# A decoder kernel on one core: other opening order, ternary weights by comparisons, and one projection piece in two parts

## The chip, the cores and the metric

The kernel runs on 1 core of one Trainium2 chip. The metric is the device time of one execution in microseconds. A profiled execution also gives a span, from the first to the last instruction that the profiler shows.

## What is computed

Sixteen sequences of 256 tokens with 512 features pass one decoder layer of three parts, each followed by adding the input and normalising (mean 0, variance 1 over the features).

```python
x = _layernorm(x + _L0_attn_ref(x, w_q, w_k, w_v, w_o), axis=-1)
x = _layernorm(x + _L0_xattn_ref(ctx, ctx, x, ssm_kernel, D, 8), axis=-1)
x = _layernorm(x + _L0_ffn_ref(x, gamma, W), axis=-1)
```

The first part is causal attention with 16 heads of 32, whose four projections are of the "bit" kind:

```python
sw = 1.0 / jnp.clip(jnp.mean(jnp.abs(w)), 1e-05, None)
wq = jnp.clip(jnp.round(w * sw), -1.0, 1.0) / sw
sx = 127.0 / jnp.clip(jnp.max(jnp.abs(x), axis=-1, keepdims=True), 1e-05, None)
xq = jnp.clip(jnp.round(x * sx), -128.0, 127.0) / sx
y = xq @ wq.T
```

So each weight matrix (512 x 512) becomes -1, 0 or 1 times its mean size, which is known only when the whole matrix has been read, and each token becomes integers times its own scale. The second part is a causal convolution of products of the context with a kernel, multiplied with the layer's input; the third is one more such projection with weights W. Both are left alone by the change, except that W's rounding lies in the first part's steps.

## The kernel before, in words

**Attention** works on one sequence (a "batch" b, 256 tokens, two tiles of 128) per step, 16 steps, in a pipeline over batches. Everything is ordered by hand: inside `manual_schedule` each of the five instruction streams (PE, ACT, DVE, POOL, SP) runs in the order in which the source issues it.

In step b the four head groups g are gone through as four rounds. A round is `scan(b+1, g)`, which computes the scores of the next batch to get the row maxima (`nmax`, L311 on DVE), some other PE work, `weigh(b, g)`, which computes the scores transposed with the maxima added (L339, L346), takes the exponential on ACT (L351), masks it on POOL (L355) and adds two parts on POOL (`both`, L361), and more PE work. `scan` and `weigh` use one and the same PSUM tile `s` (4 of 8 banks, one buffer), so a scan waits for the exponentials of the weighing before it, and a weighing for the maxima of the scan before it. `values(b, g)` multiplies probabilities with V (L374) and sums them (L381). All other PSUM tiles ("misc": `total`, `row`, `acc`, `acc_v`, `pv`, `tps`, `ops`, `acc_o`, `tpn`) share three banks in turn.

The PE work between the rounds is the projection of batch b+2: four pieces `project_qk(b+2, i)`, i = 0 and 2 for Q, 1 and 3 for K, each two blocks of 128 features (eight matmuls, L260) that DVE scales out of PSUM with one operation on 512 elements (L264), and two pieces `project_v` (L272, scaled out by ACT, L276). Piece 0 comes after scan 0, pieces 1 and 2 after the weighings 0 and 1, piece 3 after scan 3, the V pieces after scan 2 and weighing 2. Further: `spread` (the token scales as a row, L236, copied by ACT, L238), `lay` (the maxima split in three bf16 terms on DVE, L320 to L323) and `lay_turned` (their transposition on PE, L329, copied by ACT to `low`, L331; `spread` and `weigh` need `low`), `divide`, `out_scales`, `close` (the output projection, L442 to L446), `keep`. Tokens of batch b+3 are loaded, scaled on POOL (L157), rounded on ACT (L163) and transposed by a DMA (L251).

**The opening** is `begin` (L556) and `first_step` (L586), before step 0. The loads are issued first: x[0], w_k, x[1], w_o and w_f on the SP queue, w_q, w_v and two small ones on the ACT queue (L57 to L69). The constants are made on POOL where the source stands (L71 to L104); the scheduler was free to mix them there, since that part is outside `manual_schedule`. A weight matrix i lies as 128 x 2048 f32 in a buffer lent from the later `x1t` tile. It is made ternary in these steps:

1. `weight_size` (L114): the sum of the absolute values per partition, on DVE for w_q (L116) and on ACT for the others (L118).
2. `weight_scale` (L120): a matmul with ones adds over partitions (L123), DVE makes the multiplier (L124, L125), `weight_inverse` its inverse (L127).
3. `weight_round` (L132): multiply and add a magic number (L135), which rounds, then clip (L136): for w_q and w_k in halves on DVE, for the others whole on POOL.
4. `weight_store` (L145): ACT subtracts the magic number and writes bf16 (L147).

The tokens of batches 0 and 1 are turned on PE (`transposed`, L166 to L171) and their scales spread by a matmul with `diag` (L225, L234). Then `first_step` runs the four scans of batch 0, projects batch 1 and V of both, and makes w_v, w_o and a part of w_f ternary. The rest of w_o and w_f follows in step 0 (L512 to L514, L525).

**The second layer** (from L644) goes over 32 heads; nothing in it is changed.

Of the kernel before, what the change touches and what calls it, by code (L numbers as in the profile page):

```python
# [32 lines left out]
def decoder_kernel(ctx: ExitStack, tc: tile.TileContext, x, ctx_t, w_q, w_k, w_v, w_o, ker, d_skip, gamma, w_f, out):  # L33
# [25 lines left out]
    for i, w in enumerate((w_q, w_k, w_v, w_o, w_f)):  # L59
        (nc.scalar, nc.sync, nc.scalar, nc.sync, nc.sync)[i].dma_start(  # L60
            raw[i].rearrange("p (c o) -> p c o", o=E), w.rearrange("(c p) o -> p c o", p=P)
        )
        if i == 1:
            second = xp.tile([P, S // P, E], F32, name="xt")
            nc.sync.dma_start(second, x[1].rearrange("(t p) e -> p t e", p=P))
    rows = lent(6, E + P, XH)
    nc.scalar.dma_start(rows, ker)
    dsk = lent(7, 1, XH)
    nc.scalar.dma_start(dsk, d_skip.rearrange("(h o) -> h o", o=1))  # L69

    ones = const.tile([P, P], F32, name="ones")  # L71
    nc.gpsimd.memset(ones, 1.0)
    ident = const.tile([P, P], F32, name="ident")
    make_identity(nc, ident)
    ident_h = const.tile([P, P], BF16, name="ident_h")
    nc.vector.tensor_copy(ident_h, ident)
    half = const.tile([P, 2], F32, name="half")
    nc.gpsimd.memset(half, -0.5)


    mask_f = lent(7, 3 * P)[:, P : 3 * P].rearrange("p (j k) -> p j k", j=2)
    nc.gpsimd.memset(mask_f, 0.0)
    for j in range(2):
        nc.gpsimd.affine_select(
            out=mask_f[:, j, :], in_=mask_f[:, j, :], compare_op=ALU.is_ge, fill=NEG_INF,
            base=0, pattern=[[-1, P]], channel_multiplier=1,
        )
    mask = const.tile([P, 2, P], BF16, name="mask")


    pick_f = const.tile([P, NB + 1], F32, name="pick_f")
    nc.gpsimd.memset(pick_f, 0.0)
    for base in range(0, P, 8):
        if base % DH != 24:
            nc.gpsimd.affine_select(
                out=pick_f, in_=pick_f, compare_op=ALU.not_equal, fill=1.0,
                base=-base, pattern=[[-1, NB + 1]], channel_multiplier=1,
            )
# [3 lines left out]
    nc.gpsimd.memset(col, 0.0)  # L102
    for g in range(NB):
        nc.gpsimd.memset(col[:, g, g : g + 1], 1.0)  # L104
# [6 lines left out]
    parts = const.tile([P, 5], F32, name="parts")  # L111
    w_mul = const.tile([P, 5], F32, name="w_mul")

    def weight_size(i, engine):  # L114
        if engine is nc.vector:
            nc.vector.tensor_reduce(parts[:, i : i + 1], raw[i], AX.X, ALU.add, apply_absolute_value=True)  # L116
        else:
            nc.scalar.activation(lent(5, W), raw[i], AF.Abs, accum_out=parts[:, i : i + 1])  # L118

    def weight_scale(ps, i):  # L120
        total = ps.tile([P, 1], F32, name="total", tag="misc")
        c = slice(i, i + 1)
        nc.tensor.matmul(total, ones, parts[:, c], start=True, stop=True)  # L123
        nc.vector.tensor_scalar(w_mul[:, c], total, 1.0 / (E * E), 1e-5, ALU.mult, ALU.max if i < 4 else ALU.add)  # L124
        nc.vector.reciprocal(w_mul[:, c], w_mul[:, c])  # L125

    def weight_inverse(i):  # L127
        nc.vector.reciprocal(w_inv[:, i : i + 1], w_mul[:, i : i + 1])
        if i == 0:
            nc.vector.tensor_scalar(q_scale, w_inv[:, 0:1], 1.0 / math.sqrt(DH), None, ALU.mult)  # L130

    def weight_round(i, engine, part, n=2):  # L132

        both = (
            lambda t: engine.tensor_scalar(t, t, w_mul[:, i : i + 1], MAGIC, ALU.mult, ALU.add),  # L135
            lambda t: engine.tensor_scalar(t, t, MAGIC + 1.0, MAGIC - 1.0, ALU.min, ALU.max),  # L136
        )
        if n == 1:
            t = raw[i][:, part * W // 2 : (part + 1) * W // 2]
            both[0](t)  # L140
            both[1](t)
        else:
            both[part](raw[i])

    def weight_store(i, half=None):  # L145
        c = slice(0, W) if half is None else slice(half * W // 2, (half + 1) * W // 2)
# [841 lines left out]
```

## Time and profile before

| | us |
|---|---|
| median of 3 runs | 903.2 (902.22 to 903.83) |
| the profiled execution | 903.6 |
| its span | 901.3 |
| PE busy | 807.7 (90%) |
| DVE busy | 683.3 (76%) |
| POOL busy | 594.2 (66%) |
| ACT busy | 421.4 (47%) |

The profile is of one execution. Its page gives the busy time of each engine, the span in 40 slices of 22.5 us, the DMA queues, the chain of waits that ended last, and the costliest groups of instructions by source line. Apart from the page the trace answers questions: a timeline of single instructions (start, duration, engine, line, output <- input, and in brackets the idle time before it and what ended it), and windows (for each engine the busy time and, in brackets, the number of instructions, in the order PE, PEld, DVE, ACT, POOL, then the granted PE clock, the share of the DMA engines and GB/s). PEld is PE's loading of weights. An engine that is idle costs nothing where another one sets the pace.

### The profile page before, as it was taken

The page shows a single profiled execution, that of the slowest core. Times are in us where ns is not written, and L with a number is a line of the kernel's source. Part 1 is how long each engine was busy: PE and PEld are TensorE (multiplying, and loading weights), DVE is VectorE, ACT ScalarE, POOL GpSimd, SP SyncE. Part 2 cuts the span into 40 slices and gives each one's busy share as a digit, 9 for nine tenths or more (in the row PEclk, how much of TensorE's full clock was granted, in tenths as well). Part 3 has the DMA queues.
Part 4 walks back from the last instruction along what each step waited for, and adds up shares of the span by engine and source line. Part 5 has one row for each costly group of instructions (what it writes and reads, how often), then busy time and mean ns, then how long its engine had stood idle before and what let it go on. Part 6 is the DMA issues. An engine that isn't in the chain of part 4 may idle for free. (4 is left out here: it accounts for less than half of the span.)

```text
span 901.3 us, 20309 instructions
## 1 busy us (share of the span) xinstructions
PE 807.7 (90%) x7784; PEld 577.1 (64%) x7860; DVE 683.3 (76%) x1748; ACT 421.4 (47%) x696; POOL 594.2 (66%) x689
## 2 busy tenths in 40 slices
PE   3788999999999999997668999999999999999991
PEld 2456666666666666665336777777777776767770
DVE  5747777787888777876355788888888887888883
ACT  5463555556555556554442344333444334424432
POOL 3554545454544455443456999999899998998970
PEclk9999999999999999999988999999999999999995
DMA  8012223332222222111140323333223333233201
GB/s 306 1 40 67 65 72 72 71 73 45 47 66 66 67 71 72 49 36 36 38 116 12 82 75 81 86 89 94 83 75 89 84 93 77 76 83 93 65 31 34
DMA packets 103695, 64.91 MB, mean 72 GB/s; under 512 B 68080, under 2 KB 84464, under 8 KB 103600
## 3 DMA queue, kind: packets, MB, share of 16 engines
q1 hardware_dynamic: 102448, 61.45, 25.7%
q10 hardware_dynamic: 1152, 2.18, 0.7%
q8 instruction: 62, 1.02, 0.5%
q14 instruction: 33, 0.27, 0.1%
HBM read 43.34 MB, written 8.47 MB: 57 GB/s over the span
## 5 line engine op out<-in xcount | busy, mean ns | idle before, releaser
L706 PE MATMUL y<-kv,w 128*128 128x288 f32 x1280 | 336.6, 411 | 4.3 <-DVE turn L730 4.0
L706 PEld LDWEIGHTS y<-kv,w 128*128 128x128 f32 x1280 | 234.9, 191 | 65.1 <-issue 8.7
L864 POOL TENSOR_TENSOR own<-own,turn 128x512 f32<-128x512 f32 x128 | 162.9, 1272 | 35.5 <-DVE turn L730 20.2
L355 POOL TENSOR_SCALAR_AFFINE_SELECT p<-p 128x512 f32<-128x512 f32 x128 | 80.9, 656 | 139.2 <-ACT p L351 135.4
L311 DVE TENSOR_REDUCE nmax<-s 128x4 f32<-128x512 f32 (+1 forms) x128 | 116.6, 953 | 63.9 <-PE s L306 62.7
L675 POOL TENSOR_TENSOR kv<-c 128x512 f32<-128x512 f32 (+1 forms) x160 | 148.7, 947 | 2.6 <-DMA c<-in_ctx_t 2.6
L351 ACT ACTIVATE p<-s 128x1536 f32<-128x1536 f32 x64 | 92.9, 1451 | 84.4 <-PE s L346 84.4
L764 ACT ACTIVATE root<-quarter 128x3 f32<-128x3 f32 (+2 forms) x33 | 6.7, 204 | 226.1 <-DVE quarter L759 226.1
L361 POOL TENSOR_TENSOR both<-p 128x512 f32<-128x512 f32 x64 | 81.9, 1280 | 5.3
L717 DVE SCALAR_TENSOR_TENSOR own<-y,q 128x128 f32<-128x128 f32 x128 | 36.0, 281 | 61.4 <-PE y L706 53.9
L866 POOL TENSOR_TENSOR own<-own 128x256 f32<-128x256 f32 x96 | 69.8, 727 | 7.5
L739 PE MATMUL tok<-ident,own 128*128 128x128 f32 x448 | 71.4, 276 | 0.7 <-POOL own L866 0.6
L739 PEld LDWEIGHTS tok<-ident,own 128*128 128x128 f32 x448 | 55.8, 141 | 24.7 <-POOL own L866 6.2
L260 PE MATMUL acc<-xit,w 128*128 128x256 bf16 x512 | 68.4, 279 | 2.4 <-DVE x1t L135 1.3
L720 DVE TENSOR_TENSOR own<-y,q 128x384 f32<-128x384 f32 x128 | 70.0, 547 | 0.2
L730 DVE TENSOR_TENSOR turn<-y,q 128x384 f32<-128x384 f32 x128 | 69.9, 546 | 0.0
L339 PE MATMUL s<-qt,kt 32*128 32x256 f32 (+1 forms) x1024 | 60.6, 350 | 4.9 <-DVE nmax L311 4.8
L306 PE MATMUL s<-kt,qt 32*128 32x128 f32 (+1 forms) x1024 | 60.9, 352 | 0.0
L260 PEld LDWEIGHTS <-w 128*128 128x128 bf16 x512 | 46.0, 100 | 22.8 <-issue 15.4
L339 PEld LDWEIGHTS s<-qt,kt 32*128 32x128 f32 x1024 | 47.7, 186 | 19.7 <-issue 9.1
L374 PE MATMUL pv<-p,va 128*32 128x256 f32 (+1 forms) x1024 | 55.7, 332 | 5.2 <-POOL p L355 5.1
L386 ACT COPY ot<-pv 128x256 f32<-128x256 f32 x64 | 23.8, 372 | 71.9 <-PE pv L374 70.9
(136 smaller groups left out, 1320.4 us busy)
## 6 DMA issues: line engine op xcount, KB each, us to landing
xt<-in_x SPq DMA_DIRECT2D x16, 512.0 KB, 4.6
xr<-in_x SPq DMA_DIRECT2D x16, 512.0 KB, 4.9
c<-in_ctx_t SPq DMA_DIRECT2D x32, 256.0 KB, 3.3
w<-taps SPq DMA_DIRECT2D x32, 256.0 KB, 4.4
out_y<-res SPq DMA_DIRECT2D x32, 256.0 KB, 2.0
c<-in_ctx_t SPq DMA_DIRECT2D x32, 128.0 KB, 3.2
x1t<-in_w_q ACTq DMA_DIRECT2D x1, 1024.0 KB, 9.0
x1t<-in_w_v ACTq DMA_DIRECT2D x1, 1024.0 KB, 14.3
```

The costliest lines, as they stand in the source:

```text
L260: nc.tensor.matmul(acc[:, j, :], w[:, c, o * P : (o + 1) * P], m.xit[:, c].rearrange("p t k -> p (t k)"), start=(c == 0), stop=(c == NB - 1),)
L311: nc.vector.tensor_reduce(m.nmax[:, t, :, g], s[:, :, cols], AX.X, ALU.max, negate=True)
L339: nc.tensor.matmul(s[:, r, lo:hi], m.kt[rows, g, k0 : k0 + P], m.qt[rows, g, q0:S], start=(lo == 0), stop=False, skip_group_check=True,)
L351: nc.scalar.activation(p, s[:, :, 0 : 3 * P], AF.Exp)
L355: nc.gpsimd.affine_select(out=own, in_=own, compare_op=ALU.is_ge, fill=0.0, base=0, pattern=[[0, 4], [1, P]], channel_multiplier=-1,)
L361: nc.gpsimd.tensor_tensor(both, p[:, :, P : 2 * P], p[:, :, 2 * P : 3 * P], ALU.add)
L675: nc.gpsimd.tensor_tensor(kv[:, :, at : at + n * B].rearrange("p c (i b) -> p c i b", b=B), c[:, :, i : i + n, :], c[:, :, i + d : i + d + ...
L706: nc.tensor.matmul(y[:, Y0 + k * HALF : Y0 + (k + 1) * HALF], lhs, kv[:, mb, k * HALF : (k + 1) * HALF], start=(mb == 0), stop=(mb == lb),)
L720: nc.vector.tensor_tensor(own[:, 1:4, :], view(y, Y0 + AT + P, [[P, 3], [1, P]]), view(q, base + B, [[B, 3], [1, P]]), ALU.mult)
L730: nc.vector.tensor_tensor(view(t, B, [[P + B, 3], [1, P]]), view(y, Y0 + AT + P, [[P, 3], [1, P]]), view(q, base, [[0, 3], [1, P]]), ALU.mult,
L739: nc.tensor.matmul(tok[:, lb, :], lhsT=own[:, d, :], rhs=ident, is_transpose=True, start=(d == 4), stop=(d == 0))
L864: nc.gpsimd.tensor_tensor(own[:, 0:4, :], own[:, 0:4, :], turns[lb], ALU.add)
```

## The change

It has five pieces.

- **Loads.** All go on the SP queue, in the order x[0], w_q, w_k, x[1], w_v, w_o, w_f, the convolution kernel, d_skip.
- **Constants.** They are made inside `manual_schedule` in source order: `constants` first in `begin`, `zeros` (zeros of `nmax`, `terms`, `col`) after the scaling of batch 1.
- **Ternary w_q and w_k by two comparisons.** Instead of multiplying, rounding, clipping and storing, `weight_below` marks w < -size/2 (f32, on POOL; for one half of w_q on DVE) and `weight_ternary` computes (w > size/2) - mark on DVE straight into bf16. The size of w_q is taken half on DVE and half on ACT. w_v, w_o and w_f are still rounded, now in halves on POOL.
- **The order of the opening.** The size of w_o moves to the end of `first_step`, that of w_f into step 0; w_o is rounded and stored in step 0, w_f in step 1. The scales and maxima of batch 1 are taken before w_k's ternaries; Q is scaled out of PSUM later.
- **The step.** `project_qk(b+2, 0)` is done in two parts: its first block where it was, its second after the second V piece. `lay_turned(b)` stands after scan 0 of step b instead of at the end of step b-1, and `values(b-1, 3)` ahead of `spread` and the projection.

```diff
-        (nc.scalar, nc.sync, nc.scalar, nc.sync, nc.sync)[i].dma_start(
+        nc.sync.dma_start(raw[i].rearrange("p (c o) -> p c o", o=E), w.rearrange("(c p) o -> p c o", p=P))
...
+    def weight_limit(i, total, above):
+        sign = 1.0 if above else -1.0
+        nc.vector.tensor_scalar(
+            limits[:, i, above : above + 1], total, sign * 0.5 / (E * E), sign * 0.5e-5,
+            ALU.mult, ALU.max if above else ALU.min,
+        )
+    def weight_below(i, half, engine):
+        c = part_of(half)
+        engine.tensor_scalar(below[:, c], raw[i][:, c], limits[:, i, 0:1], None, ALU.is_lt)
+    def weight_ternary(i, half):
+        c = part_of(half)
+        nc.vector.scalar_tensor_tensor(
+            weights[i].rearrange("p c o -> p (c o)")[:, c], raw[i][:, c], limits[:, i, 1:2], below[:, c],
+            ALU.is_gt, ALU.subtract,
+        )
...
+    def project_qk(m, i, blocks=(0, 1), wait=False):
...
         on(scan, b + 1, 0)
-        if b == 0:
-            lay_turned(batches[0], 0)
+        on(lay_turned, b, b)
         on(fetch_x, b + 3, b + 3)
         on(fetch_again, b - 1, b - 1)
+        on(values, b - 1, NB - 1)
         on(spread, b + 2, b + 2)
-        on(project_qk, b + 2, 0)
-        on(values, b - 1, NB - 1)
+        on(project_qk, b + 2, 0, (0,))
...
         on(weigh, b, 0)
+        if b < 2:
+            weight_round(3 + b, 0)
         if b == 0:
-            weight_store(3)
-            weight_round(4, nc.gpsimd, 1)
+            weight_size(4, nc.scalar)
...
         if b == 0:
-            weight_store(4)
+            weight_scale(4, weight_total(ps, 4))
+        if b < 2:
+            weight_round(3 + b, 1)
+            weight_store(3 + b, 0)
...
         on(project_v, b + 2, 1)
+        on(project_qk, b + 2, 0, (1,))
+        if b < 2:
+            weight_store(3 + b, 1)
...
         on(close, b - 1)
-        on(lay_turned, b + 1, b + 1)
...
     def begin():
         m, n = batches[0:2]
+        constants()
         fetch_x(m, 0)
         fetch_x(n, 1)
         fetch_scales(m, 0)
         fetch_scaled(m, 0)
-        nc.vector.tensor_copy(mask, mask_f)
-        weight_size(0, nc.vector)
+        nc.vector.tensor_copy(pick, view(pick_f, 0, [[1, NB + 1], [0, P]]))
+        weight_size(0, nc.vector, 0)
+        weight_size(0, nc.scalar, 1)
+        total = weight_total(ps, 0)
+        weight_limit(0, total, 0)
+        weight_below(0, 1, nc.gpsimd)
+        weight_below(0, 0, nc.vector)
+        weight_limit(0, total, 1)
+        weight_ternary(0, 0)
+        weight_ternary(0, 1)
+        weight_scale(0, total)
         fetch_rounded(m)
         weight_size(1, nc.scalar)
-        weight_scale(ps, 0)
-        spread(m, 0)
         turn_in(m, 0)
-        for half in range(2):
-            weight_round(0, nc.vector, half, 1)
-            weight_store(0, half)
-        weight_scale(ps, 1)
...
+        spread(m, 0)
+        total = weight_total(ps, 1)
+        weight_limit(1, total, 0)
+        weight_below(1, 0, nc.gpsimd)
+        weight_below(1, 1, nc.gpsimd)
+        weight_limit(1, total, 1)
+        weight_scale(1, total)
         fetch_scales(n, 1)
         fetch_scaled(n, 1)
+        weight_ternary(1, 0)
+        weight_ternary(1, 1)
+        zeros()
+        weight_size(2, nc.scalar)
         fetch_rounded(n)
+        q0 = project_qk(m, 0, wait=True)
+        q1 = project_qk(m, 2, wait=True)
+        k0 = project_qk(m, 1, wait=True)
+        q0()
+        k1 = project_qk(m, 3, wait=True)
+        k0()
+        return q1, k1
```

The first step after it, as it stands after the change:

```python
def first_step(q1, k1):
    m, n, o = batches[0:3]
    fetch_x(o, 2)
    q1()
    k1()
    scan(m, 0)
    weight_scale(2, weight_total(ps, 2))
    turn_in(n, 1)
    spread(n, 1)
    for part in range(2):
        weight_round(2, part)
        weight_store(2, part)
    scan(m, 1)
    project_qk(n, 0)
    values_scale(m)
    values_scale(n)
    fetch_scales(o, 2)
    values_scale(o)
    fetch_scaled(o, 2)
    scan(m, 2)
    project_qk(n, 1)
    project_v(m, 0)
    project_v(m, 1)
    fetch_rounded(o)
    turn_in(o, 2)
    weight_size(3, nc.scalar)
    scan(m, 3)
    project_qk(n, 2)
    lay(m, 0)
    project_v(n, 0)
    total = weight_total(ps, 3)
    project_qk(n, 3)
    weight_scale(3, total)
    project_v(n, 1)
    write_taps()
```

## The prediction

> **What bounds the kernel now.** I read the 40 slices first: PE is at 9 tenths in nearly all of them, except the first three (0 to 68 us), the seam between attention and the second layer (425 to 475 us) and the end. The chain of waits that ends last lies in the second layer, which the change does not touch. So two places matter: the opening, and the attention steps as far as PE waits in them.
>
> The timeline of PE gives the steps by their first scan (L299).
>
> ```profile
> 23.09 0.60 PE L299 MATMUL s<-mask,ident_h 128*128 128x256 bf16 x4
> 46.74 1.06 PE L299 MATMUL s<-mask,ident_h 128*128 128x256 bf16 x4
> 51.19 0.94 PE L339 MATMUL s<-qt,kt 32*128 32x256 f32 x16
> 72.51 0.60 PE L299 MATMUL s<-mask,ident_h 128*128 128x256 bf16 x4 [1.16 <-ACT p L351]
> 225.23 0.60 PE L299 MATMUL s<-mask,ident_h 128*128 128x256 bf16 x4
> 250.69 0.60 PE L299 MATMUL s<-mask,ident_h 128*128 128x256 bf16 x4
> ```
>
> The opening takes 46.74 us; step 0 starts there. A later step takes 250.69 - 225.23 = 25.46 us. In it PE waits twice for more than a moment:
>
> ```profile
> 209.67 0.94 PE L339 MATMUL s<-qt,kt 32*128 32x256 f32 x16 [0.23 <-DVE nmax L311]
> 218.76 0.60 PE L299 MATMUL s<-mask,ident_h 128*128 128x256 bf16 x4 [0.64 <-ACT p L351]
> ```
>
> The fourth scan of a step waits 0.64 us for the exponentials, while before the first weighing PE is full (it starts at 228.92 with no wait). In the opening the windows of 2 us show PE nearly idle at 42 to 46 us, and the clock granted afterwards at 0.50; the timeline shows a 0.19 us cast that took 1.90 while POOL ran a rounding of 1.89 us.
>
> ```profile
> 42.00:44.00 2.00, 0.28 (x2) 0.01 (x1) 1.93 (x3) 0.00 (x0) 1.92 (x2) 1.00 0.00 0
> 44.00:46.00 2.00, 0.80 (x3) 0.36 (x3) 1.61 (x7) 0.89 (x2) 1.91 (x4) 0.84 0.00 0
> 46.00:48.00 2.00, 2.00 (x11) 0.90 (x13) 0.00 (x0) 1.64 (x3) 1.66 (x1) 0.50 0.32 66
> 42.34 1.90 DVE L322 CAST terms<-rest 128x40 bf16<-128x40 f32 x1
> ```
>
> **Part 1, the loads.** Before, x[0] (0.52 MB) shares the DMA engines with w_q on the other queue and lands at 6.97; w_q lands at 9.80, w_k at 13.03. Adding the MB moved in the windows of 1 us gives 0.39 by 4 us, 0.65 by 5, 1.45 by 7, 1.86 by 8, 2.59 by 10, 2.99 by 11. On one queue, served in order, x[0] is through at 4.5, x[0] and w_q (1.57) at 7.3, with w_k (2.62) at 10.1. The old landings lie about 1.0 to 1.3 behind such sums (x[0] and an equal part of w_q, 1.05 MB, are through at 6.0; landed 6.97). So I take x[0] at 5.5, w_q at 8.4, w_k at 11.4, x[1] at 13 and w_v at 15.4 (15.6 before). That one queue can carry it is seen at 18 to 19 us, when the other queue has landed its last byte (16.7): 389 GB/s. SP's load of x[2] comes behind the one of d_skip, which waits for x[0] (5.5), and waits itself for POOL's last read of x[0] (8.6); the weights queued ahead take longer.
>
> ```profile
> 18.00:19.00 1.00, 0.74 (x4) 0.56 (x5) 0.97 (x2) 1.00 (x2) 0.00 (x0) 1.00 1.05 389
> ```
>
> **Part 2, up to the first scan.** DVE: amax 1.22 and two of 0.2 from 5.5 give x_m at 7.1 (8.6 before). POOL's constants, in source order, end near 5.4 (12 selections of 0.25 from 2.3), so they delay nothing. POOL then scales x (2 x 0.7) and makes diag (2 x 0.6), to 9.8. The size of w_q: each half takes 2.29/2 on DVE and 1.91/2 + 0.19 on ACT, to 9.7. Two sums on PE (0.74 from DVE's end to the next use, and 0.28 for the second matmul): 10.7.
>
> The two comparisons have no row. `below` is a one-operand DVE operation on 1024 elements (L136: 0.69) or half of POOL's 1.97. Both start at 10.8, one on each engine; after the blocked cast above I let one wait for the other, to 12.5. The ternary combination (L154, two SBUF operands, 1024 elements) lies between 0.69 (L136, one operand) and 1.90 (the cast behind POOL); from 512 elements (L264, 0.75) and 1.1 ns for each more (L720 to L409) I take 1.25. Two of them from 12.5, then two scales: 15.4. Meanwhile ACT sizes w_k from 11.4 (1.91 + 0.19), and only then copies xit (2 x 0.55), at 14.6; the row matmul waits for the first copy (1.0) and w_k's sum follows, so the limits of w_k come at 15.8. POOL's two `below` end at 17.9, DVE meanwhile makes amax of x[1] and x_m; its two tiny ones wait out POOL, 18.4. Two ternaries: 20.9. POOL scales x[1], makes its diag (2.6) and only then the zeros (1.2): 22.3, needed by nmax at 24.2. The rest of K's projection, 0.8, and the second block, 1.05: first scan at 22.7, against 23.0. So up to here the new weights buy almost nothing: four operations of 1.25, three of 1.0 on POOL and one of 0.7 replace eight of 0.7 and four stores on ACT.
>
> The Trainium skill, "SBUF — State Buffer", section "Who interferes with whom", speaks against this: it says that a DVE instruction with two SBUF inputs is locked out while GpSimd reads SBUF, and that the first to issue holds the pair for its whole length. The blocked cast agrees for a one-operand operation; no row here shows two SBUF operands beside POOL. By that rule w_k's ternaries would alternate with POOL's two scalings of x[1] (0.7 each) and the first scan would come at an estimated 23.4 instead of 22.7.
>
> **Part 3, from the first scan to step 0.** Here DVE and ACT gain, since the size of w_o and w_f is no longer taken before w_v is stored (2 x 2.1 on ACT), and w_v is rounded and stored in halves. Before, nmax runs at 25.49, 29.33, 34.42 and 38.65. After: the scales of q1 and k1 first (to 23.9), nmax of scan 0 at 24.2 to 26.0 (amax of x[1] is already done), scan 1 at 26.4 behind turns and row, nmax 27.9 to 29.7, scan 2 at 29.9. DVE then scales q (0.75) and takes amax of x[2] (1.21 + 0.4), so nmax 2 runs 32.1 to 33.9; scan 3 at 34.1, nmax 3 to 37.5. POOL rounds w_v from 26.4 in four pieces to 30.3, ACT stores the last half by 31.4, in time for the V projection at 32.2. ACT: V evictions to 34.9, x[2] rounded to 36.2, size of w_o to 38.3. PE waits for that: sum 38.3, V eviction 39.0, last K projection to 40.1, last V to 41.1. **Step 0 starts at 41.1, 5.6 earlier.** Its first weighing starts 4.45 after its scan before, 3.69 in a later step; the 0.50 clock and the turn, copy and row one after the other made the difference. With the values laid between I take 3.4: 44.5 against 51.19, **6.7 earlier**.
>
> Steps 0 and 1 then carry w_o and w_f: 2.1 for size and 2 x 1.06 of stores on ACT in step 0 (3.8 in two stores before), 2 x 2 of rounding on POOL in each. What hides them: ACT is busy 13.9 of 26 us there (50 to 76), POOL 13.4. Behind ACT's size stand one copy of 0.37 and the next exponential, which needs a weighing that ends 3 us later. POOL's rounding (2.0) ends 0.6 or more before the next selection. If that cover were gone, each piece could cost up to its own 2 us.
>
> **Part 4, the step order, 13 times (steps 1 to 13 project).** Half a projection (0.5 on PE) leaves the stretch between scan 0 and the first weighing and lands behind the second V projection, where PE waits 0.64: all of it fits. The turn (0.11) moves behind scan 0. The first weighing was set by PE, 3.69 after its scan: 3.69 - 0.5 + 0.11 = 3.3. Next is DVE: nmax of scan 0 runs 226.77 to 228.59, right behind the moments of `close` (end 226.67), and a weighing starts about 0.15 after nmax (209.52, 209.67): 3.51, or 3.40 if the earlier scan lets nmax start 0.1 sooner. The values stand directly behind scan 0 now and need POOL's sum `both`, which ends 2.41 after the scan; PE gets there at 2.3, so it waits about 0.15 and that is still inside. The gain is 3.69 less 3.40 to 3.51, 0.2 to 0.3; afterwards all waits shift alike. DVE gains one instruction (0.45 + 0.45 for 0.75), in a stretch where it idles 2.94. Bounds: 0.1 and 0.45. 13 x 0.25 = **3.3**.
>
> **Sum.** The profiled execution took 903.6 (span 901.3), 0.4 above the median of the three runs, 903.2. 6.7 + 3.3 = 10.0; 903.6 - 10.0 = 893.6 for such an execution, **893.2** for the median. Bounds: each of the four ternaries in line by -0.55 or +0.65 (-2.2, +2.6), landings of w_q and w_k by 1 us either way, PE at 0.5 clock in the gap at 18 to 21 us (up to 0.8), steps 1.3 to 5.9: 888.5 to 899.0.
>
> **Rivals.** (a) The comparisons and POOL block each other more, or part 3 hangs longer on ACT (w_o's size before the last projections): the opening gains only 2.7; 903.2 - 2.7 - 3.3 = 897.2. For it: the blocked cast, the long queue on ACT. Against: DVE idles 2.0 to 3.5 us at a time there. (b) The ternaries run in 0.7 and loads come early: 9.5 and 13 x 0.3; 889.8. (c) The step edit does nothing, since DVE's nmax sets the first weighing anyway: 896.5. Against it: the 228.59 above. (d) **Slower**: one queue carries only what is seen at the start (170 GB/s in the window of 3 to 4 us). The 6.9 MB up to x[2] then take 40.6 us and land at 43.6; DVE, in order, holds nmax 2 behind amax of x[2], wanted at 30.5, so all after it comes 13.1 later: 906.3. It decides against the change below some 176 GB/s; 389 at 18 to 19 us speaks against it.
>
> **How the numbers follow.** Forecast 0.58, (a) 0.17, (b) 0.12, (c) 0.08, (d) 0.05. 888.5 to 899.0 takes in all but (d) and tails. About 0.2% (1.8 us) is what a measurement of this kernel can tell from no change. Slower by more: most of (d), 0.04; within: 0.03, the rest of (d) and the tail of (a); faster: 0.93.
>
> **What would show it.** x[0] landing near 5.5 and w_k near 11.4; the first scan near 22.7; step 0 near 41 with the clock at 1.00; steps of 25.1 to 25.3 with no wait above 0.2 at the fourth scan and a wait for nmax before the first weighing; L154 near 1.25. Wrong would be: PE waits for `both` over 0.3 in each step, steps 0 and 1 longer than 25.8, or x[2] landing after 30 us.

## The result, and the profile after

| | before | after |
|---|---|---|
| median of six runs each, us | 903.1 (901.5 to 903.8) | 895.8 (894.4 to 898.8) |
| the profiled execution, us | 903.6 | 897.0 |
| its span, us | 901.3 | 895.3 |
| first scan / step 0 / its first weighing | 23.09 / 46.74 / 51.19 | 26.02 / 43.12 / 46.62 |
| a later step, us | 25.46 | 25.355 |
| start of step 14 | 403.45 | 397.53 |

After takes 0.992 of the time before (95% interval 0.990 to 0.994): 7.3 us faster by the medians, where 9.9 were forecast (893.2). The time lies inside the range, 2.6 above the forecast.

The timeline of PE of the changed kernel, the lines that answer to those of before (L331 is the scan, L371 the weighing):

```profile
26.02 0.60 PE L331 MATMUL s<-mask,ident_h 128*128 128x256 bf16 x4
43.12 0.60 PE L331 MATMUL s<-mask,ident_h 128*128 128x256 bf16 x4
46.62 0.94 PE L371 MATMUL s<-qt,kt 32*128 32x256 f32 x16 [0.55 <-DVE nmax L343]
67.94 0.60 PE L331 MATMUL s<-mask,ident_h 128*128 128x256 bf16 x4 [1.60 <-ACT p L383]
213.69 0.60 PE L331 MATMUL s<-mask,ident_h 128*128 128x256 bf16 x4 [0.20 <-ACT p L383]
220.06 0.60 PE L331 MATMUL s<-mask,ident_h 128*128 128x256 bf16 x4
223.76 0.94 PE L371 MATMUL s<-qt,kt 32*128 32x256 f32 x16
245.41 0.60 PE L331 MATMUL s<-mask,ident_h 128*128 128x256 bf16 x4
```

The first scan comes 2.9 us later than before, not 0.3 earlier; step 0 still comes 3.6 earlier, because all that lies between is shorter. The wait of 0.64 at the fourth scan is down to 0.20, as forecast, and yet a step is only 0.1 shorter: the first weighing comes 3.70 after its scan, as before (3.69).

The start of step 14 is the mark by which I compare profiles: what lies behind it is the second layer, touched by no kernel here, and the last two steps, in which only the two moves apply (the last output projection ends 63.8 us behind the mark, before and after). All this took 493.1 to 497.9 us from one profile to the next, so a single span says little below 5 us. Up to it the changed kernel gains 403.45 - 397.53 = 5.9: 3.6 up to step 0, 0.95 in step 0 (25.77 to 24.82, with the clock at 1.00 where it was 0.50 to 0.84; from its scan to its turn 1.40 us instead of 2.34), and 13 x 0.105 = 1.4 in the steps. The other 1.4 us by which the medians differ is within the scatter and is put down to nothing here.

Where the opening lost time is seen in the timelines of POOL, DVE and PE from 10 to 24 us:

```profile
10.51 3.40 POOL L150 TENSOR_SCALAR x1t<-x1t,limits 128x1024 f32<-128x1024 f32 x1 [1.31 <-DVE limits L143]
15.65 5.66 POOL L150 TENSOR_SCALAR x1t<-x1t,limits 128x1024 f32<-128x1024 f32 x2 [1.74 <-DVE limits L143]
10.46 0.75 DVE L150 TENSOR_SCALAR x1t<-x1t,limits 128x1024 f32<-128x1024 f32 x1
11.31 1.95 DVE L154 SCALAR_TENSOR_TENSOR w<-x1t,limits 128x1024 bf16<-128x1024 f32 x1
13.95 1.28 DVE L154 SCALAR_TENSOR_TENSOR w<-x1t,limits 128x1024 bf16<-128x1024 f32 x1 [0.69 <-POOL x1t L150]
18.53 2.13 DVE L154 SCALAR_TENSOR_TENSOR w<-x1t,limits 128x1024 bf16<-128x1024 f32 x1 [1.31 <-POOL x1t L150]
21.35 1.70 DVE L154 SCALAR_TENSOR_TENSOR w<-x1t,limits 128x1024 bf16<-128x1024 f32 x1 [0.69 <-POOL x1t L150]
20.72 0.39 PE L290 MATMUL acc<-xit,w 128*128 128x256 bf16 x2 [1.79 <-DVE w L154]
23.11 3.08 PE L290 MATMUL acc<-xit,w 128*128 128x256 bf16 x14 [2.00 <-DVE w L154]
```

A comparison (`below`, L150) takes 0.75 on DVE and 2.83 on POOL (3.40 beside DVE's), where I had put 1.0. DVE waits for POOL ahead of three of the four ternary operations, and PE waits for DVE ahead of K's projection. Then the projection itself is slow: 14 matmuls in 3.08 us, 0.22 each, with the granted clock down to 0.51. The windows of 2 us, the PE clock in the third column from the end:

```profile
22.00:24.00 2.00, 0.89 (x5) 0.65 (x6) 1.71 (x2) 0.99 (x2) 2.00 (x2) 0.64 0.00 1
24.00:26.00 2.00, 2.00 (x11) 1.45 (x10) 1.39 (x2) 0.27 (x1) 1.83 (x13) 0.51 0.00 0
```

### The profile page after: what moved, and what is told of

Read it like the earlier page. It is cut to its first block, busy times and chain, and to the rows that moved or that the text cites. A ratio compares the mean times of both kernels' runs of the same rounds, so it can differ in the third digit from the quotient of the medians.

```text
span 895.3 us, 20336 instructions
## 1 busy us (share of the span) xinstructions
PE 811.7 (91%) x7785; PEld 576.3 (64%) x7862; DVE 687.4 (77%) x1756; ACT 419.0 (47%) x697; POOL 605.5 (68%) x698
## 5 line engine op out<-in xcount | busy, mean ns | idle before, releaser
L290 PE MATMUL acc<-xit,w 128*128 128x256 bf16 x512 | 72.1, 282 | 4.3 <-DVE w L154 3.8
L371 PE MATMUL s<-qt,kt 32*128 32x256 f32 (+1 forms) x1024 | 60.6, 350 | 5.2 <-DVE nmax L343 5.2
L371 PEld LDWEIGHTS s<-qt,kt 32*128 32x128 f32 x1024 | 47.7, 186 | 20.1 <-issue 9.3
```

Source lines behind the costliest of these rows:

```text
L290: nc.tensor.matmul(acc[:, j, :], w[:, c, o * P : (o + 1) * P], m.xit[:, c].rearrange("p t k -> p (t k)"), start=(c == 0), stop=(c == NB - 1),)
L371: nc.tensor.matmul(s[:, r, lo:hi], m.kt[rows, g, k0 : k0 + P], m.qt[rows, g, q0:S], start=(lo == 0), stop=False, skip_group_check=True,)
```

## The experiments

The theory after the result: POOL's comparisons, 1.8 us each dearer than I took them, make the opening late; in the step the turn (`lay_turned`), put ahead of the first weighing, takes back most of what the split gives: by its own 0.22 us and by starting 1.40 us after the scan, where the row started 1.29 after it (the 0.11 that the expectations call the change of rows). Rivals: the ternary operations, or what the new order and the loads do otherwise, make the opening late; in the step, the split itself gives little. Medians are of 4 to 12 runs, ratios to runs of the kernel before on the same chip; the marks from "first scan" on are from one profile of each.

| run | what differs from after | median, us | ratio to before (95%) | first scan | step 0 | per step | step 14 |
|---|---|---|---|---|---|---|---|
| after | | 895.84 | 0.992 (0.990 to 0.994) | 26.02 | 43.12 | 25.355 | 397.53 |
| e1_below_dve | comparisons on DVE | 893.20 | 0.989 (0.986 to 0.992) | 22.34 | 39.43 | 25.355 | 394.01 |
| e2_round_dve | old rounding of w_q, w_k | 890.45 | 0.986 (0.983 to 0.989) | 21.23 | 38.33 | 25.355 | 393.03 |
| e4_two_ops | comparison as two operations | 898.71 | 0.995 (0.994 to 0.997) | 28.51 | 45.74 | 25.355 | 400.16 |
| e5_busy_gap | more matmuls in the gap | 894.59 | 0.990 (0.988 to 0.992) | 24.66 | 41.75 | 25.355 | 397.56 |
| l1_old_loads | two load queues | 897.40 | 0.994 (0.992 to 0.996) | 28.03 | 45.58 | 25.355 | 400.03 |
| s1_split_only | of the step edit, the split alone | 893.58 | 0.989 (0.986 to 0.992) | 26.04 | 43.97 | 25.27 | 397.26 |
| s2_old_step | step edit undone | 897.13 | 0.993 (0.990 to 0.996) | 25.89 | 43.01 | 25.46 | 398.72 |
| s3_no_split | step edit without the split | 902.53 | 1.001 (0.999 to 1.003) | 25.88 | 43.83 | 25.86 | 404.79 |
| b1_round_split | e2 and s1 together | 889.23 | 0.985 (0.983 to 0.987) | 21.91 | 39.00 | 25.27 | 392.61 |
| b2_busy | b1 and more matmuls | 888.71 | 0.984 (0.982 to 0.986) | 21.03 | 38.13 | 25.27 | 391.69 |

### The comparisons on DVE: e1_below_dve

```diff
-        weight_below(0, 1, nc.gpsimd)
         weight_below(0, 0, nc.vector)
+        weight_below(0, 1, nc.vector)
...
-        weight_below(1, 0, nc.gpsimd)
-        weight_below(1, 1, nc.gpsimd)
+        weight_below(1, 0, nc.vector)
+        weight_below(1, 1, nc.vector)
```

> The changed kernel with all four comparisons `below` on DVE instead of three on POOL and one on DVE; the rest is the same. Theory A: a comparison of 1024 elements costs POOL 2.7 to 2.8 us by itself (15.65 to 21.31 for two in the changed kernel), DVE 0.75 (L150, 10.46); K's weights wait for POOL alone. Then the limits of w_k at 15.5 are followed by 2 x 0.75, amax of x[1] and its scales (1.6) and two ternaries of 1.28: K ready at about 21.5 instead of 23.05, first scan at about 24.3 instead of 26.0, step 0 at about 41.6 instead of 43.1, the time 1.5 us less. Rival B: what lies behind the first scan on ACT (the size of w_o before the last projections) sets step 0 anyway: the first scan is 1.7 us earlier, step 0 less than 0.5 us, the time the same within 0.5 us.

Theory A holds, not rival B: step 0 came 3.7 earlier, like the first scan. Step 14 came 3.5 earlier, more than twice the gain that the expectation had for POOL's comparisons, and the first scan at 22.34, close to the forecast's 22.7. The timelines of DVE, POOL (the first of two scalings of x[1]) and PE:

```profile
15.29 1.42 DVE L150 TENSOR_SCALAR x1t<-x1t,limits 128x1024 f32<-128x1024 f32 x2
18.28 2.46 DVE L154 SCALAR_TENSOR_TENSOR w<-x1t,limits 128x1024 bf16<-128x1024 f32 x2
18.52 2.70 POOL L185 TENSOR_SCALAR xq_t<-xt,x_m 128x512 f32<-128x512 f32 x1 [9.70 <-DVE x_m L207]
20.80 1.70 PE L290 MATMUL acc<-xit,w 128*128 128x256 bf16 x14 [0.81 <-DVE w L154]
```

Two comparisons of w_k take 1.42 here and 5.66 on POOL, and the two ternary operations 2.46, as much as those of w_q with nothing beside them (2.48). POOL's scaling, which started 0.24 behind the first of them, paid instead: 2.70 where it takes 0.69 alone. The first scan gained 3.68: PE's last 14 projections start 23.11 - 20.80 = 2.31 earlier, and take 1.70 instead of 3.08, 1.38 less. PE's gaps are 0.8 here and 1.8 and 2.0 in the changed kernel, and no window of this profile before step 14 shows less than the full clock (a column that misses some slow stretches, see the last section). That second part the expectation lacked.

### The old rounding back: e2_round_dve

```diff
-        weight_below(1, 0, nc.gpsimd)
-        weight_below(1, 1, nc.gpsimd)
...
-        weight_ternary(1, 0)
-        weight_ternary(1, 1)
+        weight_round(1, 0, nc.vector)
+        weight_round(1, 1, nc.vector)
...
+        weight_store(1, 0)
+        weight_store(1, 1)
```

(w_q likewise.)

> The changed kernel with w_q and w_k made ternary in the old way (multiply and round, clip on DVE in halves, store on ACT), the new order of everything else kept. Theory A (the comparisons as they are laid out are the slow part): 4 x (0.75 + 0.69) on DVE and 4 stores of 1.06 on ACT; K ready at about 19.5, first scan at about 21.7 instead of 26.0, step 0 at about 40, the time about 3 us less than the changed kernel. Rival C: the stores delay ACT's size of w_v by 4 us and with it the rounding of w_v and the V projections, so that step 0 stays at 43 and the time within 0.5 us.

Theory A holds: the first scan came at 21.23, 4.8 before the changed kernel's and 1.1 before e1's; step 0 is 4.8 earlier (rival C: not at all) and step 14 4.5, since step 1 took 25.65. So the two comparisons are no gain for this opening even with all of them on DVE: a matrix costs DVE 1.42 + 2.46 = 3.88 by comparisons in e1, and here 2.88 by multiplying, rounding and clipping (four operations, 14.62 to 17.50 us for w_k), while ACT stores two halves at 1.06 each. What made the changed opening faster is its order and the loads, which this run has too, not the new weights.

### The loads on two queues again: l1_old_loads

```diff
-        nc.sync.dma_start(raw[i].rearrange("p (c o) -> p c o", o=E), w.rearrange("(c p) o -> p c o", p=P))
+        (nc.scalar, nc.sync, nc.scalar, nc.sync, nc.sync)[i].dma_start(
+            raw[i].rearrange("p (c o) -> p c o", o=E), w.rearrange("(c p) o -> p c o", p=P)
+        )
...
-    nc.sync.dma_start(rows, ker)
+    nc.scalar.dma_start(rows, ker)
```

(d_skip likewise.)

> The changed kernel with the weights and constants loaded by two queues as in the kernel before, the order of all else as changed. Theory L (the order of the loads is worth what the prediction took: w_q lands near 9.8 instead of 7.9, w_k near 13.0 instead of 11.05, and the chain of limits, comparisons and projections hangs on both): first scan and step 0 about 1.9 later, time 1.9 us longer than the changed kernel. Rival R (GpSimd's comparisons, not w_k, end the opening: their first pair is released late either way): under 0.7 later. A step stays at 25.355 by both.

DVE's first work on w_q in this run and in the changed kernel, each released by the load:

```profile
9.84 1.22 DVE L130 TENSOR_REDUCE parts<-x1t 128x1 f32<-128x1024 f32 x1 [0.52 <-DMA x1t<-in_w_q]
```

```profile
7.88 1.22 DVE L128 TENSOR_REDUCE parts<-x1t 128x1 f32<-128x1024 f32 x1 [0.60 <-DMA x1t<-in_w_q]
```

w_q came 1.96 later, the first scan 2.0, step 0 and step 14 2.5. The last 0.45 is not the load's: scan 0 ran at the slow pace here (1.06 us instead of 0.60). Theory L holds: everything in the opening hangs on the first two weights, and POOL's slow comparisons come on top of the load, not instead of it.

### Why POOL compares so slowly: m1_prices, e4_two_ops, m2_pairs

> The changed kernel with a measuring stretch put behind its constants; it adds work on scratch columns and leaves nothing out, so its own time is of no interest. GpSimd runs 128x1024 f32 operations by themselves, two of each: is-less-than against a column, multiply and add, min and max, multiply alone; then VectorE's one ternary operation (greater-than and subtract, two SBUF operands) runs alone, then five of them beside two multiply-adds and two comparisons of GpSimd. Theory A (the comparison is dear by its operation: 2.8 us in the changed kernel because GpSimd compares slowly, not because it was disturbed): comparisons 2.7 to 2.9 us each alone, the other kinds 1.0 to 1.3 each as the row of the kernel before. Theory B (contention: in the changed kernel the comparisons were held by VectorE): comparisons 1.0 to 1.3 alone too, longer only beside VectorE. For the ternary operation both say 1.25 to 1.28 alone; beside GpSimd 1.7 to 2.2, by the changed kernel's rows, if GpSimd's reads slow it, 1.28 where only waits for its operand made those rows long.

The timeline of POOL: L121 is-less-than a column, L123 multiply and add, L125 min and max, L127 multiply alone, two of each and nothing beside them; L130 and L132 are multiply-add and is-less-than again, beside DVE's five ternary operations (L134), of which single ones are shown.

```profile
7.42 5.78 POOL L121 TENSOR_SCALAR x1t<-x1t,half 128x1024 f32<-128x1024 f32 x2
13.29 2.33 POOL L123 TENSOR_SCALAR x1t<-x1t,half 128x1024 f32<-128x1024 f32 x2
15.71 2.17 POOL L125 TENSOR_SCALAR x1t<-x1t 128x1024 f32<-128x1024 f32 x2
17.98 5.80 POOL L127 TENSOR_SCALAR x1t<-x1t,half 128x1024 f32<-128x1024 f32 x2
...
25.14 1.28 DVE L134 SCALAR_TENSOR_TENSOR w<-x1t,half 128x1024 bf16<-128x1024 f32 x1
25.20 2.21 POOL L130 TENSOR_SCALAR x1t<-x1t,half 128x1024 f32<-128x1024 f32 x1 [1.41 <-DVE w L128]
26.46 2.02 DVE L134 SCALAR_TENSOR_TENSOR w<-x1t,half 128x1024 bf16<-128x1024 f32 x1
...
29.56 3.69 POOL L132 TENSOR_SCALAR x1t<-x1t,half 128x1024 f32<-128x1024 f32 x1
30.57 2.02 DVE L134 SCALAR_TENSOR_TENSOR w<-x1t,half 128x1024 bf16<-128x1024 f32 x1
```

Theory A holds for the price: a comparison takes 2.89 with nobody beside it, so contention was not the cause. But a multiplication alone takes 2.90 as well, and two operations in one instruction 1.09 to 1.17: so far it is the lone operation that is dear, not the comparison.

Beside each other the two engines take turns. The multiply-add, 1.17 alone, started beside a ternary operation and ended at 27.41, 0.99 behind the other's end (26.42); the next ternary, 1.28 alone, ended at 28.48, 1.07 behind that. A comparison does not hold a ternary up for its whole length: the one of 30.57 ended at 32.59, before the comparison (33.25).

The profile of the kernel before held a sign of the price. `diag` (L225) and `v_mul` (L218) are lone multiplications on POOL:

```profile
11.18 0.61 POOL L225 TENSOR_SCALAR diag<-ident,x_v 128x128 f32<-128x128 f32 x1
32.27 0.57 POOL L218 TENSOR_SCALAR v_mul<-x_v,w_inv 128x2 f32<-128x2 f32 x2
```

From 2 to 128 elements that is 0.29 to 0.61 us, about 2.5 ns for each more, which makes an estimate of 2.8 to 2.9 us for 1024. The multiply-add that scales x took 0.7 for 512.

Next, the same comparison with a second operation:

```diff
-        engine.tensor_scalar(below[:, c], raw[i][:, c], limits[:, i, 0:1], None, ALU.is_lt)
+        engine.tensor_scalar(below[:, c], raw[i][:, c], limits[:, i, 0:1], 1.0, ALU.is_lt, ALU.mult)
```

> The changed kernel with one edit: the comparison is written as two operations of the same instruction, is-less-than and then a multiply by 1.0, on the same engines in the same places. In the measuring run a GpSimd tensor-scalar instruction of 128x1024 f32 with one operation took 2.89 to 2.90 us whether it compared or multiplied, and 1.09 to 1.17 with two operations. Theory F (the form with one operation is what is dear): the three comparisons of GpSimd take 1.1 to 1.3 by themselves and up to 2.1 beside VectorE's ternary operation, the last one ends near 18 instead of 21.3, the K ternaries near 20.5 instead of 23.05, and the first scan starts at 22.0 to 22.7 instead of 26.0 (the forecast's 22.7), step 0 at 39.2 to 40.5, the whole 3 to 4 us below the changed kernel. Rival O (comparing is dear on GpSimd in every form, and multiplying by a column alone happens to be as dear): 2.8 us each again, first scan 25.9 to 26.3, no gain.

Neither held. In its timeline of POOL the comparisons are dearer than before, 3.69 each:

```profile
16.38 7.38 POOL L150 TENSOR_SCALAR x1t<-x1t,limits 128x1024 f32<-128x1024 f32 x2 [1.74 <-DVE limits L143]
```

The first scan went to 28.5 and step 14 to 400.16, 2.6 behind the changed kernel. So a list of pairs was measured:

> The changed kernel with a measuring stretch of GpSimd behind its constants (nothing left out, its own time is of no interest): one each of eleven operations on 128x1024 f32, by itself, in this order: less-than a number; multiply by a number; max with a number; multiply by a column and add a number; multiply by a number and add a number; multiply by a column and by a number; max with a column and min with a number; less-than a column and add a number; add a column and less-than a number; less-than a column and multiply by a number; and a product of two operands. What is open after the run with the comparison in two operations (3.69 and 4.27 us where 1.1 to 1.3 was hoped for): why multiply-add and min-max are cheap (1.17, 1.09), a lone multiply or a lone comparison dear (2.90, 2.89) and a comparison with a multiply dearer. Theory P (pairs of arithmetic operations are cheap; a lone operation or a pair with a comparison in it is dear): 2.9 for the first three, 1.1 to 1.2 for the next four, 3.5 to 3.8 for the three pairs with a comparison. Theory N (a column as operand is what is dear, unless it is multiply and add): the first three 1.0 to 1.2, multiply by a column and a number and max-min with a column 2.9 or more. Theory M (only the two pairs that the rounding uses are cheap): multiply and multiply 2.9 or more, max and min with the column about 1.1.

The timeline of POOL: L119 less-than a number, alone (multiply and max alone: 2.79 and 2.77); L123 multiply and add numbers; L124 multiply by a column and a number; L125 max with a column, min with a number; L126 less-than a column and add:

```profile
7.43 2.81 POOL L119 TENSOR_SCALAR x1t<-x1t 128x1024 f32<-128x1024 f32 x1
...
17.27 1.05 POOL L123 TENSOR_SCALAR x1t<-x1t 128x1024 f32<-128x1024 f32 x1
18.41 1.13 POOL L124 TENSOR_SCALAR x1t<-x1t,half 128x1024 f32<-128x1024 f32 x1
19.64 3.71 POOL L125 TENSOR_SCALAR x1t<-x1t,half 128x1024 f32<-128x1024 f32 x1
23.44 3.72 POOL L126 TENSOR_SCALAR x1t<-x1t,half 128x1024 f32<-128x1024 f32 x1
```

All three theories are wrong in a part: P only in max-min with a column (3.71 against 1.1 to 1.2), N in the lone operations and in multiply-multiply, M in both pairs. Cheap here are multiply-add and multiply-multiply, and min-max with two numbers (1.05 to 1.17); a lone operation takes 2.8 to 2.9, and each pair with a comparison, and max-min with a column, 3.7 (this one differs from the cheap min-max in its column and in its order; the two were not tried apart). Why, no run shows. No form of the comparison that was tried is cheap on POOL.

### Half clock after a gap: e5_busy_gap

```diff
+        busy(14)
         k0 = project_qk(m, 1, wait=True)
```

`busy` issues matmuls into a PSUM tile that nobody reads.

> The changed kernel with 14 more matmuls (128x256, bf16, a result that nobody reads) on TensorE between the projections of q and those of k, where TensorE idles from 18.9 to 20.7 and from 21.1 to 23.1 in the changed kernel. Theory C (after that idle time TensorE runs at half pace: the last 14 projections take 3.08 us there and 1.70 in the run with the comparisons on VectorE, whose gaps are 0.8 each): they take 1.7 to 1.9 here, first scan 24.7 to 24.9 instead of 26.02, step 0 and the rest 1.1 to 1.3 earlier. Rival W (the pace hangs on something else, on what VectorE and GpSimd read at that time for one): 3.0 to 3.1 again, first scan within 0.2 of 26.0.

The timeline of PE, the added matmuls first; then scan 0 of step 1, a round later:

```profile
18.60 2.14 PE L596 MATMUL sums<-pick,ident_h 128*128 128x256 bf16 x14
23.12 1.70 PE L290 MATMUL acc<-xit,w 128*128 128x256 bf16 x14 [2.00 <-DVE w L154]
66.57 0.60 PE L331 MATMUL s<-mask,ident_h 128*128 128x256 bf16 x4 [1.60 <-ACT p L383]
```

Theory C holds for the opening: the same 14 projections, released at the same time (23.12), take 1.70 instead of 3.08, and the first scan is 1.36 earlier. The gain did not last: in step 1, after the wait of 1.60 that the changed kernel has too (67.94), PE ran at half clock (0.50 in the window of 68 to 70 us) and the step took 26.75 instead of 25.35. At step 14 nothing of it was left (397.56). So a half-clock stretch is worth about 1.4 us, and whether a given gap brings one is not settled by its length: 1.60 did in this run and did not in the changed kernel.

### The step edit in four combinations: s1_split_only, s2_old_step, s3_no_split

The edits, against the changed step: s1 keeps the split and puts `lay_turned` and `values` back; s2 also makes the piece whole; s3 makes only the piece whole.

```diff
-        on(lay_turned, b, b)
+        if b == 0:
+            lay_turned(batches[0], 0)
...
-        on(values, b - 1, NB - 1)
         on(spread, b + 2, b + 2)
         on(project_qk, b + 2, 0, (0,))
+        on(values, b - 1, NB - 1)
...
         on(close, b - 1)
+        on(lay_turned, b + 1, b + 1)
```

> The changed kernel with `lay_turned` at the end of the step and `values` behind the projection, as before; of the step edit only the split projection is left. Theory P (PE still sets the first weighing in the changed step: the turn costs 0.22 there and 0.11 for the change of the array's rows, the values wait 0.1 for POOL's sum): without the two moves PE reaches the first weighing 3.2 after its scan and waits for nmax until 3.5; a step takes 25.28 instead of 25.35, 13 steps 1.0 us less. Rival D (DVE's nmax sets the first weighing, and the turn's move alone gave the 0.11): the step goes back to 25.46, the time is 1.4 us more.

> The changed kernel with the whole step edit undone (whole projection piece, `lay_turned` at the end of the step, `values` behind the projection); the opening and the weights in steps 0 and 1 stay as changed. Both theories of the step: 25.46 per step, 13 x 0.107 = 1.4 us more than the changed kernel. If the step edit is worth more or less than the two traces show (contention, or steps that differ), it shows here: my forecast had 3.3 us.

> The changed kernel with the projection piece whole again, the turn of the row terms and the last group of values staying in their new places: the fourth of the four step edits' combinations, against 25.46 us per step (neither), 25.27 (split alone) and 25.355 (both). Theory P (TensorE sets the first weighing in all of them, so what stands ahead of it counts in full): the turn's 0.22 and its change of rows 0.11 come in ahead of the first weighing and leave the end of the step, less what TensorE waited there; without the split 25.46 + 0.08 = 25.54 per step, first weighing about 4.0 after the scan, and the whole 13 x (25.54 - 25.355) = 2.4 us longer than the changed kernel. Theory D (VectorE's maxima set the first weighing, so that the turn moves into a wait and costs nothing there, as the prediction had it): 25.35 or less, the same as the changed kernel.

| us per step | piece whole | piece split |
|---|---|---|
| turn and values at their old places | 25.46 | 25.27 |
| turn and values moved | 25.86 | 25.355 |

The split alone brings 0.19 per step, more than the whole edit (0.105); moving the turn and the values costs 0.085 with the split and 0.40 without it. s1 and s2 came out at the periods that theory P had for them (theory D had 25.46 for s1); s3 is beyond the 25.54 of theory P, in its direction (its first weighing comes 4.14 after the scan, 4.0 expected, and the wait of 0.63 at the fourth scan is back), so the parts do not add. The timeline of PE in s1, scan and first weighing of one step:

```profile
220.35 0.60 PE L331 MATMUL s<-mask,ident_h 128*128 128x256 bf16 x4
223.86 0.94 PE L371 MATMUL s<-qt,kt 32*128 32x256 f32 x16 [0.18 <-DVE nmax L343]
```

Here the weighing comes 3.51 after the scan and waits for DVE's maxima: the upper figure that the forecast gave for this bound. In the changed kernel it comes at 3.70 with no wait. The step 0 of s1 is 0.96 later than that of s2, though the two openings are one and the same code: its clock stayed at 0.54 until 28 us, where s2 had 1.00 from 26 us. That code reached step 0 at 43.01 to 43.97 in four profiles (the changed kernel's, s1, s2, s3), so one profile of an opening tells nothing below 1 us.

### Both findings together: b1_round_split and b2_busy

> The changed kernel with the weights of q and k rounded, clipped and stored as in the kernel before (VectorE in halves, ScalarE's store), the loads in the new order, and of the step edits only the split of the projection piece. If the two findings add: step 0 starts at 38.3 to 39.3 (38.33 with the old rounding; 0.85 more if the later start of the run with the split alone belongs to it, none if that was the clock of this one execution), 25.27 per step, the last but one step's start at 38.8 + 24.82 + 13 x 25.27 less one step = about 391.5 to 392.5, against 397.53 in the changed kernel, and a median 5 to 6 us below the changed kernel's. If they do not add (an earlier start collides with the loads of w_o and w_f in the first steps): step 1 is longer than 25.3 and the start of the last step lies at 393 or later.

> The kernel with the old rounding on VectorE, the new order of the loads and the split alone (889.23 us, its first scan at 21.91, step 0 at 39.00), with 16 more matmuls that nobody reads ahead of the projections: 10 before the sum of w_q and 6 before that of w_k. Theory C: the 32 projections, 16.30 to 21.91 for the last 30 there, run at 0.12 each from the start, end 0.3 to 0.5 behind the last store of w_k's second half (18.7) plus 14 x 0.12, and the first scan starts near 20.4, 1.5 earlier, and all behind it too: about 887.7. Rival W: no change of pace, first scan 21.9 or later by what the added matmuls hold up (at most 1), 889 to 890.

b1 is the edits of e2 and s1. They add but for 0.2 us in step 1 (25.50; e2 had 25.65): step 14 is at 392.61, just behind the 391.5 to 392.5 expected if they add, and 4.9 before the changed kernel's. b2 issues 16 more unread matmuls, 10 ahead of w_q's sum and 6 ahead of w_k's. The last 30 projections take 4.83 us instead of 5.77, and the first scan came at 21.03, not at theory C's 20.4. But e2, whose opening is the same code as b1's, took 5.19 for them and had its first scan at 21.23: of the gain of 0.9 only 0.2 to 0.4 is beyond what one and the same opening does, so theory C is not shown here. By step 14 b2 is 0.9 earlier; the medians, 889.2 and 888.7, do not tell the two apart. Both beat the changed kernel, by 6.6 and 7.1 us, as their ratio intervals show.

## Why the prediction was right, and where its sum was not

The side and the range were right; of 10.0 us forecast up to the second layer 5.9 came. In the two terms of the sum: the first weighing came 4.57 us earlier (46.62 for 51.19) where 6.7 was forecast, and the steps gave 1.4 for 3.3. That the median still lies only 2.6 above the forecast is in part luck: 1.4 of its gain is not in the two profiles up to the mark, and nothing was forecast behind it. Point by point:

- **Loads: right, a little late.** x[0], w_q and w_k came at 4.95, 7.88 and 11.05 for 5.5, 8.4 and 11.4, and l1 shows that this piece is worth 2.0 us by itself at the first scan.
- **The comparison: the step that failed.** I took POOL's `below` as "half of POOL's 1.97", 1.0. That row was multiply-add, and the lone comparison takes 2.8 (m1: 2.89). The pair of w_k ended at 21.3, not 17.9, and the ternaries at 23.05, not 20.9. `diag`, a lone multiplication whose 0.6 the prediction counts, was the nearer row. The Trainium skill, "GPSIMD Engine Reference", section "Engine selection", calls GpSimd's elementwise operations with one input roughly line-rate. Against DVE's 0.69 to 0.75 for such an operation, the pairs at 1.05 to 1.17 are not far off, the lone ones at 2.8 are.
- **The ternary operation: right.** 1.25 forecast, 1.28 measured alone. With POOL's operation ahead of it, it takes 1.70 to 2.13. The paragraph on the skill's rule was right in kind: w_k's second ternary started behind a scaling of x[1] (21.29 to 21.98) and took 1.70.
- **Half clock in the gap: in the bounds only.** I allowed up to 0.8; e1 and e5 show 1.4. With the comparisons it makes the first scan 3.3 late (26.02 for 22.7).
- **Between first scan and step 0: better than forecast**, 17.1 for 18.4: ACT ended the size of w_o 14.7 behind the first scan (15.6 forecast), and PE needed 2.3 more (2.8). PE did wait there for that size, as said, 0.56 us. So step 0 came only 2.0 late, at 43.12 for 41.1; that this makes up for 1.3 of the 3.3 is luck.
- **Step 0 and 1: right in the numbers.** The first weighing came 3.50 after its scan (3.4 forecast), and w_o and w_f are hidden: 24.82 and 25.35 us. The reason given for the 3.4 was not the one: in step 0 there are no values of a batch before to lay between, turn, copy and row still follow one another, and the 0.95 gained is the pace of PE ahead of the turn (1.40 us for 2.34); then DVE's maxima set the weighing.
- **The step edit: half the mechanism.** All of the half projection did fit in the wait of 0.64. But "3.69 - 0.5 + 0.11 = 3.3" was mis-sized: ahead of the weighing the turn costs 0.22 and starts 0.11 later than the row did, the sums over `both` wait 0.08 more, and the half piece gives 0.44, not 0.5. That makes 3.69 - 0.44 + 0.41 = 3.66, measured 3.70: PE still sets the weighing, and the 0.1 per step that is left is what the turn gave back at the end of the step (weighing 3 to the next scan 2.77 for 2.88). 1.4 us came for 3.3.

Rivals (a), 897.2, and (c), 896.5, both lie nearer the median of 895.8 than the forecast does, and neither has the cause. For (a) the opening gained 4.57 rather than 2.7, and m1 shows the comparisons slow without any blocking. For (c) the step edit did little, but because of PE, not of DVE. (The 40 slices were read a little narrowly: the fourth, too, has 8 tenths, and the seam reaches from 405 to 495 us; nothing was worked out from that.)

## What to carry to other kernels

Price an operation by a row with the same operations and operands, not by the same instruction and size: on POOL here that is a factor of 2.5 (2.89 to 1.17). A small row of the right kind, carried on by its time per element, does better than a large one of another kind. When a new order lets PE idle for 2 us or so, count the slow matmuls behind the gap as well as the gap. And when an edit has two parts, do each alone: half of this step edit was worth more than the whole, and the old rounding under the new order more than the new one.

## What was not expected of the hardware

- POOL's instruction on 128x1024 f32 takes 1.05 to 1.17, 2.8 to 2.9 or 3.7 us by which operations it holds.
- A DVE operation with two SBUF operands and a POOL operation beside it take turns. In m1 ternary operations took 2.02 (1.28 alone) beside multiply-adds of 1.96 and 2.21 (1.17 alone), each ending about 1 us behind the other's end; in e1 two ternaries back to back took 1.27 and 1.28, and POOL's scaling ended 0.48 behind the second. The Trainium skill, "SBUF — State Buffer", "Who interferes with whom", has these two contend for a port that is locked; the rows agree. But POOL's comparison of 3.69 did not lock the ternary out for its whole length.
- After PE idled for 1.8 and 2.0 us, with 0.39 of work between, matmuls took 0.22 instead of 0.12. The Trainium skill, "TensorE: Matmul & The Clock Gate", section "The HAM clock gate", has the clock follow windows of 3.4 us in which PE is judged idle or busy and which do not follow the program. That the same gap of 1.60 slowed PE in one run and not in another agrees with the second; why gaps shorter than such a window slow PE at all, no run shows. The column of the granted clock does not always show it: in e4 the last 14 projections took 3.17 (0.23 each), and in the changed kernel the 16 of q 3.57 (0.22 each), at a recorded 1.00.
